# Three step buffers and two weight tiles in an NF4 round trip beside attention and a feed-forward block

## The chip, the cores and the metric

The kernel runs on 1 core of one Trainium2 chip. The metric is the device time of one execution in microseconds. Kernels are compared by the median of several executions on the same chip. A profile is one further execution, recorded by the hardware profiler; its span runs from the first to the last instruction.

## The reference

One transformer block on x of 2048 x 1024 float32 values, everything in float32:

```python
x = x + attn(layernorm(x))      # q, k, v: three 1024x1024 products; 32 heads of 32, attention
                                # between the heads of one position (softmax over 32 heads)
x = x + ffn(layernorm(x))
# ffn, hidden width 2752:
dq = nf4_quant_dequant(w)       # for w1, w2, w3: per block of 64 values, divide by the block's
                                # absolute maximum, take the nearest of 16 codes, multiply back
h  = silu(x @ dq1.T) * (x @ dq2.T)
y  = h @ dq3.T
```

The weights w1, w2 (2752 x 1024) and w3 (1024 x 2752) come unquantized, so the round trip through the 16 codes is part of the work.

## The kernel before, in words

**Foreground.** TensorE is the main engine, and the order of its instructions is written out by hand (manual_schedule for TensorE alone, L283). The orders on the other engines (ACT, DVE, POOL and the SP queue, which issues DMAs) are set by a scheduler at build time, from the dependencies, the buffers that are free and its own estimates. On the chip each engine then works strictly in that order. First come three sweeps of eight row pairs each for q, k and v (until some 820 us), with attention beside them. Each product of two matrices is done as seven products of halves instead of eight (Strassen's scheme), by accumulating in PSUM and copying out partial sums in between: ACT copies them (copied, L358), DVE adds. Then come the feed-forward passes: six groups of up to four hidden chunks of 128, each for both halves of the rows. A Unit makes one hidden chunk: seven products, with ACT copies L895, L902, L909, activations L906 and L916, and DVE sums and products L905, L911, L917, L921, L922. At the end of a pass, down7 (L980) multiplies by w3: it accumulates in PSUM, ACT copies every partial sum out (give, L1002), and POOL issues a DMA that adds it to the running result in DRAM (L1004), 28 times in each pass. The next product on the same PSUM tile must wait for the copy. For the last group, down (L1042) loads the running result instead (L1051), adds on DVE (L1078) and stores.

**Background.** The round trip of the weights runs beside all this, as a Python generator (background, L219) that the foreground advances step by step: advance(n) takes n steps, and spent(us) takes 0.69 steps for each microsecond of TensorE work. There are 65 jobs of a 128 x 1024 tile each (the last of w3 is half as wide). For job n:

- load_w (L130) loads the weight tile wn, by a DMA on the SP queue: L142 for tiles of w1 and w2, L134 for tiles of w3, L139 and L140 for the mixed one. The tiles have the tag wn with three buffers, and the load of job n+2 is asked for when job n begins (L228).
- absmax takes the maximum of each block of 64 on DVE (L207), two small DVE instructions make the reciprocals (L214, L215), and ACT divides the tile block by block, 16 instructions of 128 x 64 (scaled, L195, "wn<-wn,rc"). It is called for job n+1 after step 9 of job n.
- 15 steps on the whole tile (L232 to L245): each compares with one bound and folds the code in. Three use DVE alone (L234, L236, L238). The other twelve are in two parts: ACT makes from the tile a clipped ramp sg (L242), and DVE folds sg into the result r (L243). The ramp sg has the pool's two buffers, so ACT can be at most two ramps ahead of DVE. The steps on r are a chain.
- the result is multiplied by the block maxima again, on ACT (L195, "r<-r,am") or in every other job of the feed-forward stage on DVE (L254).
- finish (L147) transposes r on TensorE (L161), copies it from PSUM on ACT (L162, "wop"), makes sums and differences for the seven-product scheme on DVE (L168 to L177), and stores them to DRAM (L180). From there the feed-forward units load them (L774, L775, L783, L784).

A weight tile wn is read last by the twelfth L242 of its job (L243 and the multiplication after it read only sg and r). A load into its buffer waits for that on the SP queue, in order, with everything behind it. The tag wn also serves down (L1049) for its acc tiles, after the last job is done.

Of the kernel before, what the change touches and what calls it, by code (L numbers as in the profile page):

```python
# [12 lines left out]
FP = mybir.dt.float32  # L13
# [5 lines left out]
P = 128  # L19
S = 2048  # L20
E = 1024
# [48 lines left out]
def preln_block_kernel(  # L70
# [38 lines left out]
    dqp = ctx.enter_context(tc.tile_pool(name="dq", bufs=2))  # L109
# [14 lines left out]
    jobs = []  # L124
# [4 lines left out]

    def load_w(kind, c):  # L130
        h0, hn = c * P, min(P, F - c * P)
        t = dqp.tile([P, E], FP, tag="wn", name="wn", bufs=3)
        if kind == "3":
            nc.sync.dma_start(  # L134
                t[:, : KC * hn].rearrange("p (k h) -> p k h", h=hn),
                w3[:, h0 : h0 + hn].rearrange("(k p) h -> p k h", p=P),
            )
        elif kind == "12":
            nc.sync.dma_start(t[:hn, :], w1[h0 : h0 + hn, :])  # L139
            nc.sync.dma_start(t[hn : 2 * hn, :], w2[h0 : h0 + hn, :])  # L140
        else:
            nc.sync.dma_start(t, (w1 if kind == "1" else w2)[h0 : h0 + hn, :])  # L142
        return t
# [3 lines left out]
    def finish(kind, c, v):  # L147

        hn = min(P, F - c * P)
        q = hn if kind == "3" else P  # L150
        paired = kind == "3" and c < PAIRED
        second = kind == "2" or paired and c % 2
        if not second:
            wops["t"] = dqp.tile([P, 8, 4, P], FP, tag="wop", name="wop", bufs=1)
        o = wops["t"]
        first = 2 if second else 0
        for half in range(2):
            pt = hook["psum"](half)
            for k in range(4):
                j = 4 * half + k  # L160
                nc.tensor.transpose(pt[:q, k, :], v[:, j * q : (j + 1) * q], ident)  # L161
            nc.scalar.copy(o[:q, first + half], pt[:q])  # L162
            yield
        if kind == "1" or paired and not second:
            return
        if paired:
            b11, b12, b21, b22, t1, t2, t3, t4 = (o[:, n] for n in range(8))
            nc.vector.tensor_tensor(t1, b12, b11, ALU.subtract)  # L168
            nc.vector.tensor_tensor(t2, b22, t1, ALU.subtract)
            nc.vector.tensor_tensor(t3, b22, b12, ALU.subtract)  # L170
            nc.vector.tensor_tensor(t4, b21, t2, ALU.subtract)
        if kind == "2":
            a11, a12, a21, a22, s1, s2, s3, s4 = (o[:, n] for n in range(8))
            nc.vector.tensor_tensor(s1, a21, a22, ALU.add)
            nc.vector.tensor_tensor(s2, s1, a11, ALU.subtract)
            nc.vector.tensor_tensor(s3, a11, a21, ALU.subtract)
            nc.vector.tensor_tensor(s4, a12, s2, ALU.subtract)  # L177
        n = 8 if second else 2
        d = tc.dram_tile([q, n, 4, P], FP, name=f"wd{kind}_{c}")
        nc.sync.dma_start(d, o[:q, :n])  # L180
        wd[kind, c] = d
        if paired:
            wd[kind, c - 1] = d
# [8 lines left out]
    def scaled(dst, src, by, nb):  # L192

        for n in range(nb):
            nc.scalar.mul(dst[:, ts(n, BLOCK)], src[:, ts(n, BLOCK)], by[:, n : n + 1])  # L195

    def width(kind, c):
        return KC * min(P, F - c * P) if kind == "3" else E

    def absmax(kind, c, wn):  # L200

        w = width(kind, c)
        nb = w // BLOCK
        v = wn[:, :w]
        am = fs.tile([P, 16], FP, tag="am", name="am")
        rc = fs.tile([P, 16], FP, tag="rc", name="rc")[:, :nb]
        nc.vector.tensor_reduce(  # L207
            am[:, :nb],
            v.rearrange("p (b e) -> p b e", e=BLOCK),
            AX.X,  # L210
            ALU.max,
            apply_absolute_value=True,
        )
        nc.vector.scalar_tensor_tensor(rc, am[:, :nb], 0.0, am[:, :nb], ALU.is_equal, ALU.add)  # L214
        nc.vector.reciprocal(rc, rc)  # L215
        scaled(v, v, rc, nb)
        return am

    def background():  # L219
        ready = load_w(*jobs[0])  # L220
        ahead = load_w(*jobs[1])
        am = absmax(*jobs[0], ready)
        yield
        for n, (kind, c) in enumerate(jobs):
            wn, wa = ready, am
            ready = ahead
            if n + 2 < len(jobs):
                ahead = load_w(*jobs[n + 2])  # L228
            w = width(kind, c)
            v = wn[:, :w]  # L230
            r = dqp.tile([P, E], FP, tag="r", name="r", bufs=2)[:, :w]
            for i, (side, edge, code) in enumerate(STEPS):  # L232
                if i == 0:
                    nc.vector.tensor_scalar(r, v, edge, code, ALU.is_lt, ALU.mult)  # L234
                elif side == "<":
                    nc.vector.scalar_tensor_tensor(r, v, edge, r, ALU.is_lt, ALU.max)  # L236
                elif side == ">":
                    nc.vector.scalar_tensor_tensor(r, v, edge, r, ALU.is_gt, ALU.subtract)  # L238
                else:
                    t = dqp.tile([P, E], FP, tag="sg", name="sg")[:, :w]  # L240
                    by = BIG if side == "+" else -BIG
                    nc.scalar.activation(t, v, AF.Copy, bias=-edge * by, scale=by)  # L242
                    nc.vector.scalar_tensor_tensor(r, t, code, r, ALU.min, ALU.max)  # L243
                step["n"] = i
                yield  # L245
                if i == 9 and n + 1 < len(jobs):
                    am = absmax(*jobs[n + 1], ready)
                    yield
            if hook["scale"] == "ACT" or n % 2:
                scaled(r, r, wa, w // BLOCK)  # L250
            else:
                r3 = r.rearrange("p (b e) -> p b e", e=BLOCK)
                f = wa[:, : w // BLOCK].unsqueeze(2).to_broadcast([P, w // BLOCK, BLOCK])
                nc.vector.tensor_tensor(r3, r3, f, ALU.mult)  # L254
            pending.append(finish(kind, c, r))
            yield

    bg = background()

    def advance(n):  # L260
# [270 lines left out]
    for p in range(NP):  # L531
# [19 lines left out]
        for j in range(2):  # L551
            t = work.tile([P, 32, NH], FP, tag="qd", name="qd", bufs=2)
# [70 lines left out]
    for p in range(NP):  # L623
# [12 lines left out]
        for j in range(2):  # L636
            t = work.tile([P, 32, NH], FP, tag="kd", name="kd", bufs=3)
# [75 lines left out]
    for p in range(NP):  # L713
# [32 lines left out]
        for j in range(2):  # L746
            t = work.tile([P, 32, D], FP, tag="vd", name="vd", bufs=3)
# [197 lines left out]
    def new_po():  # L945

        sums.append(sums.pop(0))
        pool, tag = sums[-1]
        return pool.tile([P, TB], FP, tag=tag, name="po")
# [92 lines left out]
    def down(g, tbp, hs):  # L1042

        full = [c for c in g if c < NFULL]
        for q in range(4):
            at = []
            for j in (1, 0):
                i = 8 * tbp + 2 * q + j
                a = dqp.tile([P, E], FP, tag="wn", name="acc", bufs=3)  # L1049
                for n in range(2):  # L1050
                    nc.sync.dma_start(a[:, ts(n, TB)], x1d[i][n])  # L1051
                at.append((i, j, a))
            for n in range(2):
                pos = []
                for i, j, a in at:
                    po = new_po()
                    for c in full:
                        nc.tensor.matmul(
                            po,
                            hs[c][j][:, ts(q, P)],  # L1060
                            w3T[c][:, ts(n, 512)],
                            start=(c == g[0]),
                            stop=False,
                            skip_group_check=True,
                        )
                    pos.append(po)
                for (i, j, a), po in zip(at, pos):
                    r = ts(j, HALF)
                    nc.tensor.matmul(
                        po,  # L1070
                        hs[NFULL][r, ts(q, P)],
                        w3T[NFULL][r, ts(n, 512)],
                        start=False,
                        stop=True,
                        skip_group_check=True,
                    )
                for (i, j, a), po in zip(at, pos):
                    nc.vector.tensor_tensor(a[:, ts(n, 512)], a[:, ts(n, 512)], po, ALU.add)  # L1078
            for i, j, a in at:
                nc.sync.dma_start(of[ts(i, P), :], a)  # L1080
# [84 lines left out]
```

## Time and profile before

| | |
|---|---|
| timed runs (median of 3) | 2488.63 us (2483.4 to 2490.14) |
| the profiled execution's own time | 2493.61 us |
| its span | 2491.8 us, mean granted TensorE clock 0.985 |
| L243, DVE, r<-sg,r | 780 instructions, 1213 ns each, 945.8 us busy |
| L242, ACT, sg<-wn | 780 instructions, 1053 ns each, 812.7 us busy |
| L195, ACT, wn<-wn,rc and r<-r,am | 1032 and 608 instructions, 340 and 341 ns each |
| L1002, ACT, acc<-z | 160 instructions, 581 ns each |
| L207, DVE, am<-wn | 65 instructions, 1205 ns each |
| load of a wn tile (512 KB), issue to landing | 63 issues of L134 and L142, median 4.5 us |
| accumulating DMA L1004 (256 KB), issue to landing | 280 issues, median 6.3 us |

The page gives for each group of instructions its busy time, the mean of one, the idle time of its engine just before it, and which instruction's end released it. Neighbours on one engine overlap by about 0.1 us in these durations: two DVE steps of 1.22 us that don't depend on each other start 1.13 us apart, dependent ones 1.26 to 1.33. A 512-wide float32 product of two 128 x 128 by 128 x 512 matrices shows as two matmul records, each 0.43 us after the one before when nothing holds them up, though each is listed with 0.59 us. A DMA is shown on the queue that issues it; its landing is told by the semaphore. "SPq X <- ACT sg" is the SP queue standing still.

### The profile page before, as it was taken

Reading aid. Unit: us, or ns where it says so; the run is one execution under the profiler, and the core shown is the slowest. Engines: PE = TensorE matmul, PEld = TensorE weight load, DVE = VectorE, ACT = ScalarE, POOL = GpSimd, SP = SyncE. Lnnn points to the kernel's source line nnn. Section 1 sums busy time; section 2 is a strip of 40 time slices with the busy share of each in tenths; the row PEclk is TensorE's granted clock in tenths of the full one; section 3 lists DMA queues with packets and bytes.
Section 4 is the critical chain, followed back from the end, with each engine's and each line's share of the span. In section 5 each row is a group of like instructions: output and inputs, shape, how many; then the busy total and the mean of one; then the engine's idle time right before and its main releaser. Section 6 shows DMA issues by size and latency. Waiting matters only on the chain.

```text
span 2491.8 us, 36722 instructions
## 1 busy us (share of the span) xinstructions
PE 2388.5 (96%) x14000; PEld 1119.1 (45%) x14000; DVE 1980.2 (79%) x2208; ACT 1611.2 (65%) x3267; POOL 278.6 (11%) x352
## 2 busy tenths in 40 slices
PE   7999999999899999999999999999999999999998
PEld 4444455545444444444444444444444444444433
DVE  7999788879988587889989799898988979871022
ACT  3556544344553378898888888889888888871200
POOL 1010000000000012030120301203012030120300
PEclk8999999999999999999999999999999999999998
DMA  8788643656669687394973949739396394862973
GB/s 309 282 313 315 243 156 123 232 211 220 208 230 313 205 287 168 118 191 153 321 171 118 191 147 302 195 110 203 144 301 162 144 198 148 289 153 72 202 269 131
DMA packets 177297, 513.90 MB, mean 206 GB/s; under 512 B 15904, under 2 KB 70176, under 8 KB 154720
## 3 DMA queue, kind: packets, MB, share of 16 engines
q1 hardware_dynamic: 136224, 438.08, 48.1%
q0 software_dynamic: 40320, 73.42, 18.2%
q8 instruction: 110, 1.80, 0.3%
q14 instruction: 67, 0.55, 0.1%
q10 hardware_dynamic: 576, 0.05, 0.0%
HBM read 283.69 MB, written 227.80 MB: 205 GB/s over the span
## 4 chain that ended last, share of the span: by engine, by line
issue 28%; PE 12%; ACT 10%; DVE 10%; DMA 7%; POOL 1%; SPq 0%; DVEq 0%; POOLq 0%; ACTq 0%
DVE r L243 7%; DMA x1d<-acc 5%; PE z L339 4%; ACT sg L242 3%; ACT wn L195 3%; PE z L989 2%; ACT acc L1002 2%; PE q L339 2%; ACT r L195 2%; PE y L989 1%; POOL x1d L1004 1%; PE rr L339 1%; DMA out_dram<-acc 1%; PE r L989 1%; DMA acc<-x1d 1%
## 5 line engine op out<-in xcount | busy, mean ns | idle before, releaser
L243 DVE SCALAR_TENSOR_TENSOR r<-sg,r 128x1024 f32<-128x1024 f32 x780 | 945.8, 1213 | 105.0 <-ACT sg L242 73.6
L242 ACT ACTIVATE sg<-wn 128x1024 f32<-128x1024 f32 x780 | 812.7, 1053 | 313.3 <-DVE r L243 299.2
L1004 POOL DMA_DIRECT2D x1d<-acc x280 | 243.3, 886 | 1283.4 <-ACT acc L1002 1137.3
L339 PE MATMUL z<-xB,w 128*128 128x512 f32 x720 | 323.8, 598 | 3.6 <-ACT u L909 1.9
L339 PE MATMUL z<-xT,w 128*128 128x512 f32 x656 | 295.9, 594 | 4.2 <-ACT u L902 4.2
L339 PE MATMUL q<-xT,w 128*128 128x512 f32 x656 | 291.6, 592 | 0.0
L195 ACT ACTIVATE wn<-wn,rc 128x64 f32<-128x64 f32 x1032 | 267.4, 340 | 22.4 <-DVE rc L215 22.4
L989 PE MATMUL z<-w,h 128*128 128x512 f32 x496 | 236.3, 605 | 21.7 <-ACT acc L1002 18.9
L339 PEld LDWEIGHTS z<-xB,w 128*128 128x128 f32 x720 | 135.0, 191 | 170.3 <-issue 153.8
L339 PEld LDWEIGHTS q<-xT,w 128*128 128x128 f32 x656 | 123.3, 190 | 149.5 <-issue 146.4
L339 PEld LDWEIGHTS z<-xT,w 128*128 128x128 f32 x656 | 122.0, 190 | 151.5 <-issue 138.7
L339 PE MATMUL z<-wT,A 128*128 128x512 f32 x384 | 178.1, 607 | 2.9 <-DVE wT L506 2.0
L339 PE MATMUL q<-wT,A 128*128 128x512 f32 x384 | 173.0, 593 | 1.6 <-DVE A L398 1.6
L339 PE MATMUL z<-wB,A 128*128 128x512 f32 x320 | 152.1, 620 | 13.1 <-ACT u L358 13.1
L195 ACT ACTIVATE r<-r,am 128x64 f32<-128x64 f32 x608 | 154.6, 341 | 13.8 <-DVE r L243 13.5
L989 PEld LDWEIGHTS z<-w,h 128*128 128x128 f32 x496 | 92.4, 192 | 138.6 <-issue 98.3
L989 PE MATMUL y<-w,h 128*128 128x512 f32 x320 | 149.9, 598 | 1.3 <-DVE h L968 1.1
L339 PE MATMUL rr<-xB,w 128*128 128x512 f32 x328 | 147.5, 592 | 0.0
L207 DVE TENSOR_REDUCE am<-wn 128x16 f32<-128x1024 f32 (+1 forms) x65 | 78.3, 1205 | 53.4 <-ACT r L195 47.5
L1002 ACT COPY acc<-z 128x512 f32<-128x512 f32 x160 | 92.8, 581 | 34.6 <-PE z L989 26.3
L339 PEld LDWEIGHTS q<-wT,A 128*128 128x128 f32 x384 | 71.9, 190 | 88.9 <-issue 83.0
L339 PEld LDWEIGHTS z<-wT,A 128*128 128x128 f32 x384 | 71.4, 192 | 83.2 <-issue 80.0
(132 smaller groups left out, 2592.1 us busy)
## 6 DMA issues: line engine op xcount, KB each, us to landing
x1d<-acc POOLq DMA_DIRECT2D x280, 256.0 KB, 6.3
wd<-wop SPq DMA_DIRECT2D x31, 2048.0 KB, 7.6
w<-wd SPq DMA_DIRECT2D x41, 1280.0 KB, 7.8
wn<-in_w_dram SPq DMA_DIRECT2D x63, 512.0 KB, 4.5
xT<-xdT SPq DMA_DIRECT2D x28, 1024.0 KB, 8.9
xB<-xdB SPq DMA_DIRECT2D x24, 1024.0 KB, 6.8
w<-wd SPq DMA_DIRECT2D x42, 512.0 KB, 4.8
w<-wd SPq DMA_DIRECT2D x10, 1536.0 KB, 7.2
```

The costliest lines, as they stand in the source:

```text
L195: nc.scalar.mul(dst[:, ts(n, BLOCK)], src[:, ts(n, BLOCK)], by[:, n : n + 1])
L207: nc.vector.tensor_reduce(am[:, :nb], v.rearrange("p (b e) -> p b e", e=BLOCK), AX.X, ALU.max, apply_absolute_value=True,)
L242: nc.scalar.activation(t, v, AF.Copy, bias=-edge * by, scale=by)
L243: nc.vector.scalar_tensor_tensor(r, t, code, r, ALU.min, ALU.max)
L339: nc.tensor.matmul(dst, w[:, k, :], xop[:, k, :], start=start and k == 0, stop=stop and k == 3, skip_group_check=True,)
L989: nc.tensor.matmul(dst, side[n][:, ts(q, P)], w3T[g[2 * m]][:, W3[n]], start=start and m == 0, stop=stop and m == 1, skip_group_check=True,)
L1002: nc.scalar.copy(t, src)
L1004: nc.gpsimd.dma_start(x1d[8 * tbp + 2 * q + j][n], t, accum_op=ALU.add)
```

## The change

Three things are changed together. The ramp sg gets three buffers instead of two. The weight tiles wn get two instead of three. And the load of job n+2 is asked for at the end of job n, after its last step, instead of at its beginning. The acc tiles of down move from the tag wn to the tag sg, so that the SBUF in use stays the same: five tiles of 128 x 1024 over both tags.

```diff
@@ load_w @@
-        t = dqp.tile([P, E], FP, tag="wn", name="wn", bufs=3)
+        t = dqp.tile([P, E], FP, tag="wn", name="wn", bufs=2)
@@ background @@
             wn, wa = ready, am
             ready = ahead
-            if n + 2 < len(jobs):
-                ahead = load_w(*jobs[n + 2])
             w = width(kind, c)
...
-                    t = dqp.tile([P, E], FP, tag="sg", name="sg")[:, :w]
+                    t = dqp.tile([P, E], FP, tag="sg", name="sg", bufs=3)[:, :w]
...
             pending.append(finish(kind, c, r))
+            if n + 2 < len(jobs):
+                ahead = load_w(*jobs[n + 2])
             yield
@@ down @@
-                a = dqp.tile([P, E], FP, tag="wn", name="acc", bufs=3)
+                a = dqp.tile([P, E], FP, tag="sg", name="acc", bufs=3)
```

## The prediction

> **What bounds the kernel now.** I read the page's first two parts, then the stages, then the waits of the one stage that the change can touch.
>
> ```profile
> span 2491.8 us, 36722 instructions
> PE 2388.5 (96%) x14000; PEld 1119.1 (45%) x14000; DVE 1980.2 (79%) x2208; ACT 1611.2 (65%) x3267; POOL 278.6 (11%) x352
> ```
>
> TensorE is the bound: eight passes of a 512-wide product take 3.43 us from start to start (0.43 each) with hardly a gap. Only its stops can be won or lost. Tables by stage, from the first pass through the feed-forward groups on:
>
> ```profile
> 900.00:2240.00 1340.00, 1305.43 (x3298) 586.80 (x3297) 1167.64 (x1268) 1137.53 (x2311) 219.18 (x252) 1.00 0.68 190
> 919.00:967.00 48.00, 44.68 (x110) 19.68 (x109) 32.15 (x32) 43.03 (x94) 20.95 (x25) 1.00 1.07 211
> 967.00:1068.00 101.00, 100.49 (x261) 45.70 (x260) 93.26 (x105) 83.45 (x171) 0.00 (x0) 1.00 0.37 127
> 1068.00:1120.00 52.00, 48.85 (x125) 21.68 (x124) 42.47 (x46) 46.92 (x91) 23.29 (x27) 1.00 1.03 215
> ```
>
> The columns are PE, PEld, DVE, ACT and POOL busy, granted clock, DMA share, GB/s. Between the down products PE idles 0.5 of 101 us. In each down stage (some 50 us, nine times, POOL busy with the accumulating DMAs) it idles 3.2 to 3.3 us; ACT is 90% busy there and the DMA engines are full (1.03 to 1.07). The modelled end of a matmul hides about 0.16 us of each stop, so I counted from the starts in the timeline: 29 stops over 0.6 us between 900 and 2240 us, 37.0 us in sum, 27 of them (33.6 us) waiting for a copy on ACT. The waits of this stage:
>
> ```profile
> DVE r L243 <- ACT sg L242: 72.9, 63, 6.8
> DVE am L207 <- ACT r L195: 43.3, 18, 4.0
> ACT sg L242 <- DVE r L243: 140.3, 207, 5.6
> PE z L989 <- ACT acc L1002: 21.2, 17, 2.3
> ```
>
> ACT and DVE wait for each other (columns: total us, times, longest). ACT is in order: a copy L1002 queued behind an L242 that waits for a free sg is late, and PE stops. In 13 of the 27 stops (14.8 us) an L242 had waited 0.2 us or more for L243 shortly before the copy.
>
> **Part 1: a third sg.** No instruction is added or removed (multisets equal on every engine; orders of PE and POOL identical). But the scheduler, given the buffer, spends it: ahead of the k-th L1002 on ACT stand on average 1.32 more L242 than before (of L902 1.80, of L909 1.51). A copy behind the i-th L242 used to need step i-2 on DVE, now i-3; so 1.0 of the 1.32 places is paid by the buffer and 0.3 is not (0.4 us at the 1.33 us pace of L243). DVE's own additions (L905 to L922) stand 0.7 to 1.1 steps later among the L243. What is gained is on DVE: its sg comes one place earlier. Of the 72.9 us, one step of 1.33 us at most is covered per wait; summed wait by wait that is 41 us. If the 14.8 us of stops shrink alike, 14.8 x 41/73 = 8 us. Bounds: nothing (the new order eats the buffer) to 15 us (all those stops go). I take **6 us won**, nearer to the lower half for the 0.3 places unpaid. In the attention stages the offset is exactly +1 at nearly all copies, so a copy needs the same step as before: nothing either way.
>
> **Part 2: two weight tiles, loaded at a tile's end.** The SP queue holds the same 65 tile loads after the same L242 counts, and a load still waits for the same event, the twelfth L242 of a tile. But the tile that it brings is one earlier: its first reader, the L207 on DVE, comes one tile sooner. Measured over jobs 17 to 63, from issue to that L207: median 33.1 us before; from the same instants to the L207 that becomes the reader, median 6.45 us (2.8 to 9.4). I add 0.4 us, since L207 moves 0.33 steps later in DVE's order, and 1.3 us, since L242 may run one step earlier: 8.2 us median. What a load takes:
>
> ```profile
> DMA to landing us min/median/max: 3.8/4.2/18.8
> DMA to landing us min/median/max: 3.4/5.6/11.6
> ```
>
> (first the w3 tiles of L134, then those of L142). The median is hidden. The tail is not, and it lies where the DMA engines are full:
>
> ```profile
> 1077.93 0.38 SPq L134 DMA_DIRECT2D wn<-in_w_dram  x1
> 1083.60 1.22 DVE L207 TENSOR_REDUCE am<-wn 128x16 f32<-128x1024 f32 x1
> 1083.73 1.06 ACT L242 ACTIVATE sg<-wn 128x1024 f32<-128x1024 f32 x1 [0.45 <-DVE r L243]
> 1084.69 0.57 ACT L1002 COPY acc<-r 128x512 f32<-128x512 f32 x1
> 1087.29 0.58 ACT L1002 COPY acc<-z 128x512 f32<-128x512 f32 x1 [2.03 <-DMA x1d<-acc]
> ```
>
> This load took 18.8 us. Changed, the L207 at 1083.6 needs it. With both corrections the loads that come late are those at 1078 (18.8 us to landing against 7.0 us of lead: 11.8 late), 1401 (16.6 against 6.6: 10.0), 1237 (10.9 against 6.2: 4.7), 1557 (9.8 against 6.5: 3.3), and two by 0.9 and 0.8: 31 us; without the 1.3 us, 43 us. DVE is in order, so behind the waiting L207 stands the next L243 (third step of the tile in the new order); ACT's sixth L242 needs exactly that step with three buffers; and behind it stand the next copy L1002 and nine more of the down stage. So DVE, ACT and PE stop in one line. PE has about 2 us of cover (one 1.72 us product beside the one that waits), leaving 9.8 + 8.0 + 2.7 + 1.3 = 21.8 us. Against that, with no copies there are no accumulating DMAs, the engines drain and the load lands sooner; how much no row shows. Bounds: 4 us (the two long ones land like the shorter ones) to 31 us (no cover, no draining). I take **16 us lost**. Nothing else moves that matters: the acc tiles of L1049 change tag after the last tile is done, the SP queue waits at the same places, and after 2240 us only PE's own work is left.
>
> A page speaks against this part. "DMA: Bandwidth & Descriptors", section "Rules for kernel authors", says that a DMA is overlapped by issuing it early, computing, and waiting late; this change issues it as late as it can. The same page's table under "Measured" has 64 KB at 0.95 us and 1 MB at 6.15; between them 512 KB would take some 3.4 us, an estimate from that page, less than any lead but the shortest, and by it part 2 would cost next to nothing and the sum would be 6 us won. The 18.8 us in the trace decides.
>
> **Sum.** The profiled execution took 2493.6 us (span 2491.8 and 1.8 around it), 5.0 above the median of the three timed runs, 2488.6. 2493.6 - 6 + 16 = 2503.6; by the median, 2488.6 + 10 = 2498.6, so I forecast **2499 us**.
>
> **Rivals.** (a) *The two parts cancel.* The full DMA engines drain as soon as the copies stop, so a late load costs 8 us in all, and the third buffer wins 6: +2, 2491 us. For it: half of the late sum is two loads. Against it: they fall into a stage that is full for 50 us. This is also the case in which the change doesn't do what it says, because the order moved L242 ahead by the place that the buffer gave. (b) *The buffer wins (the other side).* Loads land as the median does, 4.2 to 5.6 us, under the 8.2 us lead; all 14.8 us of stops behind a waiting L242 go: 2488.6 - 14.8, about 2474 us, or 2478 with one late load of 4 us. For it: 140 us of ACT's waiting and 73 us of DVE's are just what a buffer between them is for. It decides if no more than one load in the nine down stages lands after 8 us. Against it: five did in this trace (18.8, 16.6, 10.9, 9.8 and 8.1 us). A smaller gain, 8 us, gives 2480.
>
> **How the numbers follow.** Forecast (slower, around 2499, up to 2511 with 31 lost and 8 won): 0.41. (a): 0.35. (b): 0.24. The range takes in (a) whole, the undiscounted loss, and most of (b): 2476 to 2513. The forecast's own range is 2496 to 2513. A measurement of this kernel can tell about 0.3% (7.5 us) from no change; faster by more 0.24, within 0.35, slower by more 0.41.
>
> **What would show it.** Right: waits "DVE am L207 <- DMA wn" of some 25 to 40 us where there were none after 900 us, single ones of 5 to 12 us inside down stages, each followed by L242 waiting for L243 and PE waiting for L1002; and DVE's wait for L242 down from 73 to 30 to 45 us. Wrong: no wait on wn over 2 us (then the lead was enough, and (b) holds); DVE's wait for L242 unchanged (then part 1 does nothing); PE idle time in the down stages unchanged although L207 waits (then DVE had more slack than I read); or new stops in the attention stages.

## The result, and the profile after

The changed kernel takes 2494.0 us (median of 14 runs, 2487.4 to 2504.9) against 2487.6 us of the kernel before (14 runs, 2481.9 to 2495.0): **6.4 us slower**, a ratio of 1.003 with a 95% interval of 1.0019 to 1.004. The forecast was 10 us slower, with a range of 2476 to 2513. So the direction and the rough size held. The place did not, as the rest of this document shows.

The two recorded executions do not show the 6.4 us, and it is well to know why before any line is read. After's own time was 2491.9 us, 2 below its median; before's was 2493.6, 6 above its median. By their spans the changed kernel looks 1.7 us *faster*. Lines below are renumbered by the change: L240 and L241 are the former L242 and L243, the ramp sg on ACT and its folding into r on DVE. First the head of the page of after:

```profile
span 2490.1 us, 36750 instructions
...
PE 2383.9 (96%) x14000; PEld 1114.9 (45%) x14000; DVE 1983.2 (80%) x2208; ACT 1607.5 (65%) x3267; POOL 278.0 (11%) x352
```

The work is the same to the instruction on the engines. The stage of the down products, in the same window as before (us, busy time of PE, PEld, DVE, ACT and POOL, clock, DMA share, GB/s):

```profile
900.00:2240.00 1340.00, 1305.09 (x3294) 584.69 (x3293) 1169.89 (x1268) 1132.16 (x2308) 219.86 (x252) 1.00 0.68 190
```

PE was busy 1305.4 us of this window before and is busy 1305.1 us now: the stage is neither better nor worse. The waits of the same window (total us, times, longest):

```profile
ACT sg L240 <- DVE r L241: 126.0, 168, 4.0
...
DVE r L241 <- ACT sg L240: 63.3, 45, 6.5
...
DVE am L207 <- ACT r L195: 28.9, 11, 5.0
...
PE z L989 <- ACT acc L1002: 24.8, 18, 5.0
...
ACT wn L195 <- DVE rc L215: 16.4, 10, 2.8
...
DVE am L207 <- DMA wn<-in_w_dram: 7.6, 6, 3.8
```

ACT and DVE wait for each other less (140.3 to 126.0 and 72.9 to 63.3 us), but the second is far from the 30 to 45 us that the prediction named. DVE now does wait for late weight tiles, but for 7.6 us and not for 25 to 40. New is that ACT's division waits for the reciprocal (3.0 us before, 16.4 now): with a ramp more in hand, ACT reaches the division sooner than DVE has the reciprocal. The loads, first the w3 tiles of L134, then those of L142:

```profile
DMA to landing us min/median/max: 3.8/5.4/8.2
DMA to landing us min/median/max: 3.4/4.0/12.5
```

The long landings of before on L134 (18.8 us) are gone, and that is the first thing to explain. The second is where 6.4 us are lost, if not in this stage.

### The profile page after: what moved, and what is told of

It is laid out like the page before. It is cut to its first block, busy times and chain, and to the rows that moved or that the text cites. A ratio compares the mean times of both kernels' runs of the same rounds, so it can differ in the third digit from the quotient of the medians.

```text
span 2490.1 us, 36750 instructions
## 1 busy us (share of the span) xinstructions
PE 2383.9 (96%) x14000; PEld 1114.9 (45%) x14000; DVE 1983.2 (80%) x2208; ACT 1607.5 (65%) x3267; POOL 278.0 (11%) x352
## 4 chain that ended last, share of the span: by engine, by line
PE 20%; DVE 17%; issue 16%; ACT 9%; DMA 6%; POOL 1%; DVEq 0%; SPq 0%; POOLq 0%; ACTq 0%
DVE r L241 10%; PE z L339 7%; PE z L989 4%; DMA x1d<-acc 3%; ACT sg L240 3%; PE q L339 3%; ACT wn L195 2%; PE y L989 2%; PE rr L339 2%; ACT acc L1002 1%; ACT r L195 1%; DMA wd<-wop 1%; PE r L989 1%; POOL x1d L1004 1%; DVE r L234 1%
## 5 line engine op out<-in xcount | busy, mean ns | idle before, releaser
L241 DVE SCALAR_TENSOR_TENSOR r<-sg,r 128x1024 f32<-128x1024 f32 x780 | 946.2, 1213 | 95.9 <-ACT sg L240 63.7
L240 ACT ACTIVATE sg<-wn 128x1024 f32<-128x1024 f32 x780 | 806.8, 1055 | 276.3 <-DVE r L241 262.6
L1004 POOL DMA_DIRECT2D x1d<-acc x280 | 244.1, 884 | 1284.3 <-ACT acc L1002 1153.3
L989 PEld LDWEIGHTS z<-w,h 128*128 128x128 f32 x496 | 92.2, 192 | 142.8 <-issue 96.0
L207 DVE TENSOR_REDUCE am<-wn 128x16 f32<-128x1024 f32 (+1 forms) x65 | 78.2, 1203 | 52.1 <-ACT r L195 30.1
L1002 ACT COPY acc<-z 128x512 f32<-128x512 f32 x160 | 93.3, 585 | 36.8 <-PE z L989 24.5
L162 ACT COPY wop<-ptw 128x512 f32<-128x512 f32 (+1 forms) x130 | 75.7, 584 | 54.0 <-PE ptw L161 48.8
```

What stands on the lines that cost most here:

```text
L207: nc.vector.tensor_reduce(am[:, :nb], v.rearrange("p (b e) -> p b e", e=BLOCK), AX.X, ALU.max, apply_absolute_value=True,)
L989: nc.tensor.matmul(dst, side[n][:, ts(q, P)], w3T[g[2 * m]][:, W3[n]], start=start and m == 0, stop=stop and m == 1, skip_group_check=True,)
L1002: nc.scalar.copy(t, src)
L1004: nc.gpsimd.dma_start(x1d[8 * tbp + 2 * q + j][n], t, accum_op=ALU.add)
```

## The experiments

All ratios are against the kernel before on the same chip, with 95% intervals. Three theories were at stake. **A** is the prediction's: loads asked for at a tile's end come late where the DMA engines are full, and DVE, ACT and PE stop in one line. **B**: the loss is at the seam between the sweeps for q and k, near 280 us, where the trace of after shows a stop that before has not. The rival to both, C in the later expectations, leaves the DMA engines out: the moved orders cost the time. Each expectation words its theories itself.

**1. Part 2 alone** (two weight tiles and the late load, but two ramps).

```diff
-  t = dqp.tile([P, E], FP, tag="sg", name="sg", bufs=3)[:, :w]
+  t = dqp.tile([P, E], FP, tag="sg", name="sg")[:, :w]
-  a = dqp.tile([P, E], FP, tag="sg", name="acc", bufs=3)
+  a = dqp.tile([P, E], FP, tag="wn", name="acc", bufs=2)
```

> Part 2 alone: two weight tiles, loads asked for at a tile's end, but two ramps sg as before. Theory A (late loads, as predicted): L207 waits for wn some 8 us between 900 and 2240 us and TensorE loses with it in the down stages, 2490 to 2495. Theory B (one stop at the seam between the q and the k sweep): the SP queue has the order of the changed kernel there, TensorE waits about 7 us for ql near 275 us, once, and the ratio to before is about 1.003 (2494). Theory C (the third ramp buffer moved L242 ahead of the copies on ACT, and that costs): the ratio is 1.000.

Measured: 2528.2 us, 1.0164 [1.0142, 1.0187]; 40 us lost, where the prediction had 16 for this part and the expectation of A here, 2490 to 2495, at most 7. (The last group has one acc tile less; its stretch after the last down pass began took 189 us, against 186 before, so that explains some 3 us.) The mechanism in the down stages is the one predicted. Waits of the window 900 to 2240 us:

```profile
PEld z L989 <- ACT acc L1002: 65.5, 44, 12.2
DVE r L241 <- ACT sg L240: 61.5, 61, 6.1
DVE am L207 <- DMA wn<-in_w_dram: 61.4, 12, 10.4
```

And the line of stops that the prediction drew, in the timeline of this kernel, one engine after the other (SP's queue, DVE, the last work of ACT, then PE; start, duration, what, and in brackets the idle time before it):

```profile
1079.51 0.32 SPq L180 DMA_DIRECT2D wd<-wop  x1
1079.95 0.44 SPq L134 DMA_DIRECT2D wn<-in_w_dram  x1
```

```profile
1100.15 1.22 DVE L207 TENSOR_REDUCE am<-wn 128x16 f32<-128x1024 f32 x1 [10.45 <-DMA wn<-in_w_dram]
```

```profile
1092.06 0.59 ACT L1002 COPY acc<-z 128x512 f32<-128x512 f32 x1
1093.66 0.59 ACT L1002 COPY acc<-y 128x512 f32<-128x512 f32 x1 [1.01 <-DMA x1d<-acc]
```

```profile
1090.89 3.79 PE L989 MATMUL z<-w,h 128*128 128x512 f32 x8
...
1106.02 3.44 PE L989 MATMUL z<-w,h 128*128 128x512 f32 x4 [11.33 <-ACT acc L1002]
```

The load takes 20.2 us; DVE stands still for 10.45 us, ACT has nothing to copy after 1094.3, and PE stops for 11.33 us. The size follows by the prediction's own method: 61.4 us of waiting less 2 us of cover for each of 12 waits is 37 us. From the first down pass to the start of the last, this kernel took 1434 us and before 1396: 38 us. (This recorded execution is 10 us above its kernel's median, before's 6, so the down stages' share of the 40 us may be some us smaller.) So A holds for part 2 by itself. Then why not in the changed kernel?

**What the third ramp does to the loads.** The SP queue of after at the same place:

```profile
1075.01 0.38 SPq L134 DMA_DIRECT2D wn<-in_w_dram  x1
1076.21 0.32 SPq L180 DMA_DIRECT2D wd<-wop  x1
```

In before and in part 2 alone, the load stands 0.44 us *behind* the 2 MB store L180; in after it stands *ahead* of it, 2.9 us earlier than in before, and lands in 7.2 us instead of 18.8. DVE reaches L207 with no wait at all:

```profile
1081.24 1.22 DVE L241 SCALAR_TENSOR_TENSOR r<-sg,r 128x1024 f32<-128x1024 f32 x1
1082.37 1.21 DVE L207 TENSOR_REDUCE am<-wn 128x16 f32<-128x1024 f32 x1
```

What precedes each load on SP can be read in every kernel. Of the 13 recorded landings over 12 us after 900 us (fourteen kernels, the two of the case among them), 8 are loads issued 0.4 us behind an L180, 4 stand 2.2 to 5.2 us behind one, and one 6.8 us. In the kernels with three ramps and no other change to the order (after and experiments 2, 3, 8, 9 and 10), no load after 900 us follows an L180 within 6 us, and no recorded landing takes over 9.3 us (all 66 are recorded in after, in experiment 8 only 26). Each kernel with two ramps and the same order otherwise (before and experiments 1, 4, 7, 11 and 12) has loads 0.4 us behind an L180. The place alone is not enough (loads 2.2 us behind a store outside the down stages land in some 6.5 us, and four of experiments 5 and 6 that stand 0.4 us behind one in 8.1 to 9.5), but over 12 us it is needed with hardly an exception; from 10.9 to 11.7 us five loads landed with no store within 10 us ahead. That ties the long landings to the place behind the store; moving the store alone was not tried. The Trainium skill's page "DMA: Bandwidth & Descriptors", section "Two DMAs through the same engine are not ordered", says that descriptors on one queue of one DMA engine start in order. These landings agree with it.

**2. The seam mended** (the changed kernel, but the last weight chunk for v is asked for before the last products of the q sweep, not after them).

```diff
+  if not more:
+      weight_chunk("v", 3)
   cs = products(now.A, fill, ...)
...
-  weight_chunk("kv"[p // 4], p % 4)
+  if more:
+      weight_chunk("kv"[p // 4], p % 4)
```

> The changed kernel with the last weight chunk of the q sweep (its loads from wvT, L514) asked for before that sweep's last products instead of behind them; all else as changed. Theory B: the wait of TensorE for ql near 275 us is gone, about 7 us less than the changed kernel, ratio to before 1.000 (2488), 0.998 at best. Theories A and C: no difference to the changed kernel, ratio 1.003.

Measured: 2498.4 us, 1.0038 [1.0023, 1.0052]: nothing won. In after, PE at the seam:

```profile
270.29 3.60 PE L339 MATMUL q<-wT,A 128*128 128x512 f32 x8
281.10 1.78 PE L419 MATMUL sc<-kd,ql 32*32 32x32 f32 x128 [7.21 <-DMA ql<-qD]
282.81 5.88 PE L339 MATMUL z<-wT,A 128*128 128x512 f32 x8
```

A stop of 7.2 us for ql, and after it eight passes listed with 5.88 us instead of 3.6. With the seam mended this wait is gone and the first scores start at 274.0 instead of 281.1 us. But the next stop opens 20 us later. PE and ACT of the mended kernel:

```profile
289.32 1.79 PE L419 MATMUL sc<-kd,ql 32*32 32x32 f32 x128
294.85 5.82 PE L339 MATMUL z<-wB,A 128*128 128x512 f32 x8 [3.74 <-ACT u L358]
```

```profile
288.16 3.08 ACT L240 ACTIVATE sg<-wn 128x1024 f32<-128x1024 f32 x3
291.08 2.30 ACT L195 ACTIVATE wn<-wn,rc 128x64 f32<-128x64 f32 x9
293.22 1.10 ACT L586 ACTIVATE pr<-pr 128x1024 f32<-128x1024 f32 x1
294.17 0.62 ACT L358 COPY u<-z 128x512 f32<-128x512 f32 x1
```

The copy that PE needs stands behind three ramps and nine divisions on ACT. I first took this run as the fall of B. It isn't a clean test: the mending replaced one stop by others, the longest 3.7 us and again with a slow product behind it. What this does to B is told with the table at the end of this section.

**3 and 4. The third ramp alone, and its control.** A third ramp does not fit beside three weight tiles. Room was made by taking one buffer from x1 and two from accp, the tiles into which ACT copies the partial sums; the control takes the same from the kernel before.

```diff
-  x1 = work.tile([P, E], FP, tag="x1", name="x1", bufs=3)
+  x1 = work.tile([P, E], FP, tag="x1", name="x1", bufs=2)
-  accp = ctx.enter_context(tc.tile_pool(name="accp", bufs=6, ...))
+  accp = ctx.enter_context(tc.tile_pool(name="accp", bufs=4, ...))
   # part 1 alone, not the control:
-  t = dqp.tile([P, E], FP, tag="sg", name="sg")[:, :w]
+  t = dqp.tile([P, E], FP, tag="sg", name="sg", bufs=3)[:, :w]
```

> Part 1 alone: three ramps sg, three weight tiles, loads asked for at a tile's beginning; to find the room, accp has four tiles instead of six and x1 two instead of three, so it is read against the control with the same two cuts. Theories A and B: not slower than the control, up to 8 us faster; no wait of TensorE for ql near 275 us. Theory C: slower than the control by about 6 us.

> Control for part 1 alone: the kernel before with accp of four tiles instead of six and x1 of two instead of three. Every theory: 0 to 0.6% slower than before, the cost of the two cuts; no wait of TensorE for ql near 275 us.

Measured: 2542.0 us, 1.0213 [1.0192, 1.0234], and 2541.9 us, 1.0216 [1.0198, 1.0234]. The smaller pools cost 53 us, and ACT then waits some 90 us over the whole run for accumulating DMAs to free an acc tile. In this frame the third ramp is worth nothing, which says little of the original frame: another wait rules.

**5 and 6. L207 held back in DVE's order**, behind the fifth L241, in the changed kernel and in the kernel before, to give each load more time.

```diff
+  if i == 5:
+      hold = last                      # the DVE instruction of this step
...
-  am = absmax(*jobs[n + 1], ready)
+  with tc.issue_after(hold.ins):
+      am = absmax(*jobs[n + 1], ready)
```

> The changed kernel with L207 and the two instructions behind it held behind the fifth L243 of the running tile in DVE's order (1.3 steps before the edit, 5 with it): some 5 us more lead for each load. Theory A (what is left of the late loads makes the changed kernel slower): no wait of L207 for wn over 1 us between 900 and 2240 us, ratio to before 1.000 or below (2480 to 2488). Theory C (the third buffer moved L242 ahead of the copies on ACT, which costs): waits for wn gone as well, but the ratio stays at 1.003 (2495). Either: if the divisions on ACT now come too late for the next tile, DVE waits for L195 at its first steps instead, and the time goes up.

> Control for the hold: the same edit on the kernel before. There is no late load to lose there. The 43 us that L207 waits for the multiplications L195 should go; 0.996 to 1.002 of before. If this moves as much as the hold on the changed kernel does, the hold itself and not the lead is what it shows.

Measured: 2522.5 us, 1.0132 [1.0114, 1.015], and 2556.2 us, 1.0282 [1.0267, 1.0296]. The hold costs more than it could win, because the divisions, which need L207, come late too: DVE's first step then waits for them, from 900 to 2240 us 62.6 us in 35 waits in the kernel before and 24.8 us in 18 in the changed one. So these two runs don't answer what lead the loads need. The hold costs the changed kernel some 27 us and the kernel before 68; which of the changed kernel's parts makes the difference was not tried.

**7, 8 and 9. The parts in a roomier frame.** accp keeps five of six buffers, x1 two, and si shares the tag of u4. In this frame stand the control, part 1 alone, and both parts.

```diff
-  accp = ctx.enter_context(tc.tile_pool(name="accp", bufs=6, ...))
+  accp = ctx.enter_context(tc.tile_pool(name="accp", bufs=5, ...))
-  si = hp.tile([P, TB], FP, tag="si", name="si")
+  si = hp.tile([P, TB], FP, tag="u4", name="si")
   # and x1 with 2 buffers
```

> Control for it: the kernel before with accp of five tiles, x1 of two, si in the tile of u4. Every theory: between before and the first control, 0 to 1.5% over before.

> Part 1 alone with milder cuts for its room: three ramps sg and three weight tiles, accp five tiles instead of six, x1 two instead of three, si in the tile of u4; read against the control with the same cuts. Theory A: up to 8 us faster than the control, with DVE waiting less for L242. Theory C: about 6 us slower than the control. If the same: the third ramp buffer is worth nothing by itself and pays only for what two weight tiles cost.

> The changed kernel (three ramps, two weight tiles, late loads) with the same milder cuts as part 1 alone had: it fills the fourth corner, next to the control (1.0131) and part 1 alone (1.0091). If part 2 still has a price when the third ramp is there: 1.014 to 1.018, that is 12 to 22 us over part 1 alone; the price of the whole change over the control is then 0.1 to 0.5%, as it is without the cuts. If the third ramp hides all of part 2: 1.009.

Measured: control 2519.6 us, 1.0131 [1.0115, 1.0146]; part 1 alone 2510.2, 1.0091 [1.0077, 1.0105]; both 2519.1, 1.0122 [1.0107, 1.0137]. So **the third ramp wins 9 us, and part 2 beside it loses 9 us**. DVE's wait for the ramp, first in the control, then with part 1, both from 900 to 2260 us:

```profile
DVE r L243 <- ACT sg L242: 92.2, 70, 6.1
```

```profile
DVE r L243 <- ACT sg L242: 74.2, 52, 6.5
```

18 us of 92 are covered, a fifth. With both parts, the wait for late tiles is small here too:

```profile
DVE am L207 <- DMA wn<-in_w_dram: 9.4, 5, 3.7
```

**10 and 11. Light accumulation.** L1004 adds only the first 128 of each 512 columns, in the changed kernel and in the kernel before; three quarters of the running sum are not updated. (The expectation calls this "a quarter left out"; what is kept is a quarter.) The instructions stay, the DMA engines are no longer full.

```diff
-  nc.gpsimd.dma_start(x1d[8 * tbp + 2 * q + j][n], t, accum_op=ALU.add)
+  nc.gpsimd.dma_start(x1d[8 * tbp + 2 * q + j][n][:, :P], t[:, :P], accum_op=ALU.add)
```

> The changed kernel with a quarter of each accumulating DMA L1004 left out but for its first 128 of 512 columns, so three quarters of the running sum in DRAM are not updated: the 16 DMA engines are no longer full in the down stages. Theory A (late loads make up the loss): L207 does not wait for wn between 900 and 2240 us, and the kernel is as fast as the light form of before or up to 9 us faster. Theory C (the order of L242 and the copies): still some 6 us slower than the light form of before.

> Control: the kernel before with the same columns left out of the accumulating DMAs. Every theory: faster than before by what ACT waits for the acc tiles and their DMAs in the down stages, 0 to 25 us (2463 to 2488).

Measured: changed 2468.5 us, 0.9921 [0.9908, 0.9935]; before 2470.3 us, 0.9924 [0.9911, 0.9938]. The two are now the same. The DMA share around the second down pass, first of before as it is, then of the kernel before with light sums:

```profile
1065.00:1120.00 55.00, 51.85 (x132) 22.96 (x131) 45.47 (x50) 49.92 (x104) 23.29 (x27) 1.00 1.01 212
```

```profile
1065.00:1120.00 55.00, 52.96 (x136) 23.63 (x135) 44.65 (x47) 51.69 (x105) 21.71 (x26) 1.00 0.53 92
```

With 0.53 instead of 1.01, two loads directly behind an L180 still take 9.5 and 9.7 us, against a median of 4.2 for L134: by subtraction, an estimate, the store accounts for some 5 us of a long landing, and the accumulating DMAs for the other 5 to 11.

**12. Three am tiles in the kernel before**, so that L207 can run further ahead without touching the weight tiles.

```diff
-  am = fs.tile([P, 16], FP, tag="am", name="am")
+  am = fs.tile([P, 16], FP, tag="am", name="am", bufs=3)
```

> The kernel before with three buffers instead of two for am, the 16 block maxima of a tile (64 bytes in each partition), so that L207 need not wait for the multiplications L195 that still read the am of two tiles ago. If those 43 us of DVE's waits are part of what makes copies late: 0.994 to 0.999 of before. If the scheduler spends the buffer on running L207 and the divisions a tile ahead, in front of copies: same or slower.

Measured: 2493.8 us, 1.0021 [1.0008, 1.0035]. DVE's wait for the ramp falls more than with the third ramp, and the kernel still gets slower. Its waits from 900 to 2240 us:

```profile
DVE am L207 <- DMA wn<-in_w_dram: 30.8, 11, 9.2
...
PE z L989 <- ACT acc L1002: 28.2, 16, 10.8
...
ACT wn L195 <- DVE rc L215: 25.1, 10, 10.1
...
DVE r L243 <- ACT sg L242: 19.9, 29, 2.5
```

The 53 us fewer of waiting on DVE (72.9 to 19.9) do not reach PE. At least the longest wait for a late tile does: at 1092 us the 9.2, 10.1 and 10.8 us above are one line of stops, from L207 through the division to PE, and the load behind it took 18.9 us, 0.4 us behind an L180. No version that does the whole work beats the kernel before.

**Where the 6.4 us are.** The order of PE's work is written out, so the same products can be timed in each kernel. From the traces, start in us of the second group of scores, of the first product of the feed-forward groups, of the first and of the last down pass, and the span:

| kernel | 2nd scores | first feed-forward | first down | last down | span |
|---|---|---|---|---|---|
| before | 290.8 | 782.1 | 910 | 2306 | 2491.8 |
| light sums, before (11) | 286.7 | 778.2 | 903 | 2281 | 2466.0 |
| three am (12) | 286.2 | 779.1 | 905 | 2307 | 2490.6 |
| roomier control (7) | 286.4 | 778.2 | 911 | 2328 | 2512.8 |
| roomier, part 1 (8) | 289.0 | 780.8 | 913 | 2323 | 2505.7 |
| after | 292.1 | 784.8 | 910 | 2308 | 2490.1 |
| seam mended (2) | 284.0 | 783.6 | 910 | 2310 | 2494.7 |
| light sums, changed (10) | 291.4 | 784.6 | 910 | 2282 | 2465.9 |
| roomier, both parts (9) | 290.9 | 786.1 | 921 | 2333 | 2515.6 |

Read by pairs. *Part 1* (7 to 8): 2 us later at the first down pass, then 1410 us to the last instead of 1417, 7 won in the stage for which it was forecast. *Part 2 beside it* (8 to 9): **8 us later at the first down pass**, and only 2 lost after it. *Both, light sums* (11 to 10): 7 later at the first down pass, 6 won back in the stage, net nothing. *Both* (before to after): +2 in the stage; and the recorded execution of before is itself 4 us late by 291 us against its near relatives (11, 12, 7), with a granted clock of 0.95 in the first 280 us where all others compared here have 0.97 or 0.98. Set against 903 to 905 us, after is 5 to 7 us late at the first down pass. So the loss lies in the first 910 us and not in the down stages.

**The seam, product by product.** The order of PE's products is the same in all kernels here, so each product can be set against its twin. With light sums the changed kernel is 4.4 us *ahead* of its twin at the product that starts at 275 us in kernel 11, and 4.8 us *behind* at the one that starts at 295: 9.2 us are lost within 20 us, and at the first down pass it is 7.2 behind. The same stretch costs 9.5 us from 12 to after and 9.1 from 8 to 9. So theory B has the place. The stop itself comes from the order of the SP queue. At the seam it loads the last weight chunk for v (L514), writes the differences that DVE makes of it back to DRAM (L521), and loads ql, the tiles of q that the scores need (L618). First before, then after:

```profile
208.82 5.10 SPq L514 DMA_DIRECT2D cB<-in_wvT_dram  x4
...
262.86 0.93 SPq L618 DMA_DIRECT2D ql<-qD  x2
```

```profile
246.55 4.26 SPq L514 DMA_DIRECT2D cB<-in_wvT_dram  x4
...
267.41 1.52 SPq L521 DMA_DIRECT2D wtDv<-cB  x2
...
271.20 1.62 SPq L618 DMA_DIRECT2D ql<-qD  x3
```

```profile
SPq L521 <- DVE cB L517: 15.6, 1, 15.6
```

In before, the chunk stands on SP right behind a weight load of the old order (at 207.6 us); in after it comes 38 us later. DVE makes its differences between the steps of the round trip, and the whole SP queue stands still 15.6 us for L517, with the ql loads behind it. They are issued at 271.2 us, with PE's last product before the scores starting its eight passes at 270.3, and take 9.8 to 11.4 us. Every kernel with part 2 and this order (after and experiments 1, 5, 9 and 10) stops there for 6.7 to 7.2 us; so does experiment 6, without part 2, for 9.5 us, and its queue stands still in the same way (14.2 us). The other kernels without part 2 have no such stop. Why the scheduler chose this order was not traced.

Two things stay open. With the ql loads in time (experiment 2), PE is 5.2 us ahead of kernel 11 at 270 us and still 3.2 behind at 300, by stops of 1.1 and 3.7 us for copies on ACT, a slow product after the second, and smaller ones. So the order of SP is shown to cause the one stop, but that mending it wins the time back is not shown. And in the roomier pair (8 to 9) only 1.9 of the 8 us are there after the seam; the others come between 600 and 850 us, and what causes them was not traced.

## Why the prediction was right or wrong

**What bounds the kernel: right.** The stops of PE decide; work was the same on all engines.

**Part 1, 6 us won: right in size in one frame, less so in its reasoning.** In the roomier frame it won 9.4 us by the medians, 7 of them in the down stages; in the frame of experiments 3 and 4 it won nothing. The wait that was to be covered, DVE's for the ramp, shrank by a fifth (92.2 to 74.2) and not by the 41 us of 73 that were summed wait by wait; that sum took all other waits as fixed, and they weren't (ACT's for the reciprocal rose from 3.0 to 17.4 us in that pair). "In the attention stages ... nothing either way" failed by about 2 us (780.8 against 778.2 at the first feed-forward product, one recorded execution each).

**Part 2, 16 us lost: the mechanism shown, the size wrong both ways.** Alone it costs 40 us, by the line of stops that was drawn. Beside the third ramp it costs 9 us in the roomier frame, nearly all of them before the down stages. The step that failed is this one: *"The SP queue holds the same 65 tile loads after the same L242 counts ... Nothing else moves that matters."* The counts were the same, but the place of a load among the *other* DMAs of its queue was not. I carried the 18.8 and 16.6 us landings over from the old trace as if they belonged to the stage. They belonged to the place 0.44 us behind a 2 MB store in that stage. The third ramp let the twelfth L242 end sooner, the load was put ahead of the store, and the lead of 7.4 us was enough for a landing of 7.2. The leads themselves were forecast well: a median of 8.2 us for jobs 17 to 63, and 7.8 measured in after. The landings were not. (Slips in the sum of late loads nearly cancel: the leads were counted from the end of the issuing instruction and the landings from its start, 0.38 us apart, and the load at 1557 us had a lead of 5.6 and not 6.5 us, the corrections included. Redone, the sum is 30 us instead of 31.)

**Only jobs 17 to 63 were counted**, and the words "the SP queue waits at the same places" were not checked at the q/k seam. There it failed, with the 15.6 us for L517, and there PE stopped 7.2 us for ql. The leads of the first 900 us were not measured against their landings either, but that matters less: of DVE's two waits for a weight tile there in after, the one of 7.5 us at 285 us has a twin of 5.6 us in before, and at the one of 6.7 us at 522 us PE's products fall no further behind those of before and of kernel 11. The prediction's last sign, "new stops in the attention stages", is the one that fired.

**The sum, +10 against +6.4: right, but partly by luck.** A loss of 16 in the down stages and a gain of 6 were forecast. In the roomier frame it was a gain of 9, a loss of 8 before the first down pass and 2 after it, in sum about nothing, and in the original frame 6.4 us more than nothing. That difference between the frames is not explained. That the sum of two wrong places came near the measured time is luck.

**The rivals.** (a), the cancelling, is nearer by size (2491 against 2499 for 2494 measured), and its mechanism as given, late loads that cost only 8 us because the engines drain, is not what happened: the loads were hardly late. (b) had its condition met, only one recorded load in the down stages landed after 8 us (8.1), and its gain still didn't come: stops behind a waiting ramp didn't all go, and new ones stood in their place (PE's waits for L1002 on this tile went from 21.2 to 24.8 us).

**How far the wrong signs bear.** "No wait on wn over 2 us" was nearly met (the longest 3.8). "PE idle time in the down stages unchanged" was met (1305.4 and 1305.1 us busy). In the roomier frame 7 us were won there by part 1 and only 2 lost by part 2; why the two cancel in the original frame is open.

## What to carry to other kernels

A long landing time can belong to a place in a queue, and not only to a stage: before it is carried over into a forecast, look at what was issued just ahead of it, and whether the change moves the load past that. Fewer buffers and a later load are paid in lead time, so compare lead with landing over the *whole* run, and each queue's order at each seam: what stands at its head and waits holds up the loads behind it, here for 15.6 us. A buffer added elsewhere can change that order by itself. And where the order on one engine is fixed, time the same instructions in each trace: it finds in one table the stretch where a loss lies, and it shows when a recorded execution is itself off.

## What the runs showed of the hardware that I had not expected

**A stop costs more than its length.** The granted clock in the long stop of part 2 alone, in windows around it:

```profile
1090.00:1103.00 13.00, 4.69 (x11) 1.63 (x9) 2.85 (x4) 3.24 (x5) 3.45 (x4) 0.84 1.01 190
1103.00:1109.00 6.00, 2.98 (x4) 1.41 (x5) 3.31 (x4) 4.89 (x18) 1.73 (x2) 0.50 0.24 27
1109.00:1112.00 3.00, 3.00 (x11) 1.51 (x10) 0.40 (x1) 2.46 (x4) 0.86 (x1) 1.00 0.98 126
```

After 11.3 us without work PE starts at half the clock, and four passes are listed with 3.44 us instead of 1.88. From start to start a pass then takes 0.85 us instead of 0.43. Between 900 and 2300 us there are 19 such intervals (within 0.01 us) in part 2 alone and 11 each in before and after: 8 more at 0.42 us are 3.4 us of the 40. At the seam of after it is the same (a stop of 7.2 us, then a granted clock of 0.61 from 281 to 289 us and 5.88 us for eight passes instead of 3.6), while after the stop of 2.1 us in before eight passes are listed with 3.70 us. The Trainium skill's page "TensorE: Matmul & The Clock Gate", section "What's actually happening", has a clock that halves once the array has idled for a window of some 3.4 us. These stops agree.

**The same 512 KB load** takes 4.2 us in the median, 9.5 us behind a 2 MB store with the DMA engines half full, and 15.1 to 20.2 us behind it with them full.

**One buffer fewer of the six** for the partial sums' copies, with one fewer of x1 and a shared tag for si, costs 31 us (1.3%); a second one fewer, without the shared tag, costs 53 us. A pool that looked ample was near its bound.
